# A graph convolution on one core: 528 instead of 512 chunks of edges counted by source and type, one row buffer fewer, and the first ring additions and flush placed earlier

## The chip, the cores and the metric

The kernel runs on one core of a Trainium2 chip. A core has a matrix engine (TensorE, "PE" in the profile; its weight loads are listed apart as "PEld"), a vector engine (VectorE, "DVE"), a scalar engine (ScalarE, "ACT"), a general-purpose engine (GpSimd, "POOL") and a queue that does little else than issue transfers (SyncE, "SP"). They work at the same time and wait for each other through semaphores. Data lies in HBM, in the on-chip SBUF (128 partitions) and, for matmul results, in PSUM. The metric is the device time of one execution in microseconds (us); lower is better.

## The reference

A graph has 12,500 nodes with 128 float32 features each, and 200,000 directed edges with a type from 0 to 3. The node features are normalized and cut at zero. Every edge takes the row of its source, multiplies it by the 128 x 128 matrix of its type, adds that type's bias, and the results are summed per destination node and added to the input.

```python
xs = x[src]                                   # x here: relu(layernorm(x))
for i in range(4):
    mask = (edge_types == i)[:, None]
    msgs = msgs + jnp.where(mask, xs @ W[i] + b[i], 0.0)
out = jax.ops.segment_sum(msgs, dst, num_segments=N)
return x + out
```

Two facts of the inputs shape the kernel. The edges come sorted by destination, and the destination is drawn as 12,500 times a squared uniform number: low nodes have very many edges each, high nodes few.

## The kernel before, in words

The 200,000 edges are cut into 1563 chunks of 128. Because the multiplication is linear, the kernel first sums source rows per destination and type, and multiplies by the four matrices afterwards. It sums in two ways.

*The dense head.* The first `C0` = 512 chunks belong to the lowest 1392 nodes or so. For each such node the kernel counts how many edges come from which source and of which type. `count` (lines 938 to 992) does this with one-hot matrices. A "slot" is one chunk's share of one node. For every slot DVE makes two one-hots (lines 957 and 961 or 965) and PE multiplies them (line 983) into a 128 x 396 table of counts in PSUM; ACT copies it out (line 989). `multiply` (lines 1021 to 1072) then multiplies the counts with the whole table of normalized rows. The table has 98 blocks of 128 rows, each row as three bf16 parts (768 bytes), and streams from HBM through `STREAM` = 4 buffers of six blocks (576 KB each, line 1029, issued by SP). Nodes with few edges share a "unit" of up to three, told apart by powers of 256 in the counts. A batch has up to `UB` = 27 units, 12 columns each (324 columns), and every batch streams the whole table: 98 x 3 = 294 matmuls at line 1033. Four small matmuls per tail (line 1047) apply the type matrices, and DVE adds the result to `acc` (line 1066).

*The gathered rest.* The other 1051 chunks go in groups of `G` = 16. For each chunk POOL gathers 128 rows of the table by an indirect transfer (line 544) into a tile `hm` of the pool `rows` (12 buffers, two chunks each). DVE makes a one-hot of destination and type (line 561). PE adds the rows up in three matmuls per chunk (line 578, one for each bf16 part), ACT copies the sums (line 581), PE applies the four type matrices (lines 596, 603, 605), and DVE adds each chunk's piece into a ring of 2048 node columns (`ring_adds`, lines 651 to 668, one addition per chunk at line 666). The first `RAW` = 3 groups are gathered from x itself (line 528) while the table is still being made, and their sums wait in `raw_sums`.

*The order.* Until the table stands, a scheduler of the language orders the instructions. The loop at line 1304 fixes the order of PE, DVE and ACT by hand. For every group `gi` it issues the next group's gathers, and walks through the present group in parts of two chunks; before each part it puts in dense work until the share that `pace` (line 1079) asks for is reached. `pace` counts matmul columns and spreads the dense columns evenly, so that every group from the fourth to the one before the last full one has the same number of columns, own and dense together. DVE's small pieces (`side`: ring additions, one-hots, table preparation) are spread over the same parts. The additions of the raw groups join `side` at lines 1309 and 1310, one raw group in each of the groups 4, 5 and 6 (counted from zero).

*Flushes.* When all edges of a stretch of nodes have passed, `put_out` (line 704) moves that stretch from the ring to the output: PE transposes (line 691), DVE adds x, SP stores; the first flush adds the ring's first columns to `acc`. `goes` (lines 741 to 744) chooses the group after which each flush goes; the first can go no earlier than after group `RAW` + 2 = 5.

*The tables of slots.* `prep_dense` and `make_slots` (line 793) work out on the chip, while the row table is made, which rows of which chunk belong to which slot. They treat the dense chunks in blocks of 128 (`DENSE` = 4 blocks), and the slots in pieces of up to 512 columns; for each piece and block DVE makes a one-hot (line 816).

Of the kernel before, what the change touches and what calls it, by code (L numbers as in the profile page):

```python
# [35 lines left out]
F32 = mybir.dt.float32  # L36
# [12 lines left out]
P = 128  # L49
# [3 lines left out]
SG = 4  # L53
WIN = 32
ROOM = 6
C0 = 512
UB = 27
MANY = 16
HB = 6
# [7 lines left out]
RAW = 3  # L67
# [7 lines left out]
def kernel(  # L75
# [22 lines left out]
    assert NT * WIN == P  # L98
    DENSE = -(-C0 // P)
    E0 = C0 * P  # L100
    TM = T - C0
    BM = -(-TM // P)
    BR = 16
    BC = -(-TM // BR)
    assert C0 % 16 == 0 and C0 <= NFULL

# [13 lines left out]
    FULL = (TM - sum(ends_in)) // G  # L120

    def window_of(c):

        m = min((c - C0) // G, FULL)
        end = (C0 + (m + 1) * G if m < FULL else T) * P / E
        a_node = E * ((end**2 + 1 / N) ** 0.5 - end)
# [19 lines left out]
    for i, n in enumerate(sizes_of):  # L146
# [4 lines left out]
        of = alone[3 * many_at : 3 * (many_at + n1)]  # L151
# [79 lines left out]
    flag = const.tile([P, 1], I32, name="flag")  # L231

    mid = ExitStack()
    hpool = mid.enter_context(tc.tile_pool(name="rows", bufs=12))
    opool = mid.enter_context(tc.tile_pool(name="onehots", bufs=2))
    spool = mid.enter_context(tc.tile_pool(name="typed", bufs=2))
    x_ps = mid.enter_context(tc.tile_pool(name="x_ps", bufs=4, space=PSUM))
# [28 lines left out]
    QB = max(2, DENSE)  # L266

    def prep_edges(m0, m1, prep, QB):
        n = m1 - m0
        c0, c1 = C0 + m0 * P, min(C0 + m1 * P, T)  # L270
        si = prep.tile([P, QB, P], I32, name="si")
        edge_rows(si, src, c0, c1, 0)
        ty = prep.tile([P, QB, P], I32, name="ty")
        edge_rows(ty, etype, c0, c1, NT)
        di = prep.tile([P, QB, P], I32, name="di")
        edge_rows(di, dst, c0, c1, N - 1)
        if c1 > NFULL and REST:
            r = (NFULL - c0) % P
            nc.sync.dma_start(
                di[r : r + 1, n - 1, REST:], dst[E - (P - REST) :].rearrange("(p e) -> p e", p=1)  # L280
            )
        sf = prep.tile([P, QB, P], F32, name="sf")
        nc.vector.tensor_copy(sf[:, :n], si[:, :n])
        pg = x_ps.tile([P, QB, P], F32, name="pt")
        for q in range(n):
            nc.tensor.transpose(pg[:, q, :], sf[:, q, :], ident)
        nc.scalar.copy(srcT[:, m0 % TURN : m0 % TURN + n, :], pg[:, :n, :])
        nc.vector.tensor_copy(head[:, m0:m1], di[:, :n, 0])
        rel = prep.tile([P, QB, P], F32, name="si")
        for q in range(n):  # L290
            nc.vector.tensor_scalar(rel[:, q, :], di[:, q, :], head[:, m0 + q : m0 + q + 1], None, ALU.subtract)
        key = prep.tile([P, QB, P], F32, name="sf")
        for q in range(n):
            nc.vector.scalar_tensor_tensor(
                key[:, q, :], ty[:, q, :], span[:, m0 + q : m0 + q + 1], rel[:, q, :], op0=ALU.mult, op1=ALU.add
            )
        pk = x_ps.tile([P, QB, P], F32, name="pt")
        for q in range(n):
            nc.tensor.transpose(pk[:, q, :], key[:, q, :], ident)
        nc.scalar.copy(keyT[:, m0 % TURN : m0 % TURN + n, :], pk[:, :n, :])  # L300
        nc.vector.tensor_reduce(ends[:, m0:m1, 0], rel[:, :n], AX.X, ALU.max)
        nc.vector.tensor_sub(ends[:, m0:m1, 0], ends[:, m0:m1, 0], span[:, m0:m1])
        nc.vector.tensor_reduce(ends[:, m0:m1, 1], rel[:, :n], AX.X, ALU.min)
# [34 lines left out]
    nc.vector.memset(warm, 0.0)  # L338
    nc.scalar.activation(warm, warm, AF.Sqrt)
    prep_edges(0, 1, prep, QB)  # L340


# [386 lines left out]
    def due(jb):  # L729
# [7 lines left out]
    sizes = [G] * FULL + ([r] if r else []) + ends_in  # L737
    starts = [sum(sizes[:i]) for i in range(len(sizes))]

    final = len(sizes) - 1  # L740
    goes = [
        next((i for i in [*range(RAW + 2, FULL), final - 1] if starts[i] + sizes[i] >= c), final)
        for ja, _, c in flushes
    ]

# [520 lines left out]
    for g in groups:  # L1266
# [17 lines left out]
    raw_adds = [  # L1284
        ring_adds(m * G, G, lambda i, m=m: raw_sums[:, (m * G + i) * win_raw : (m * G + i + 1) * win_raw], win_raw)
        for m in range(RAW)
    ]
# [9 lines left out]
    rows = gather(RAW * G, G)  # L1297
# [6 lines left out]
    for gi, (t0, g) in list(enumerate(zip(starts, sizes)))[RAW:]:  # L1304
        q = (t0 + 8 * G) // P
        if (t0 + 8 * G) % P < G and 2 <= q < BM:
            steps = [prep_steps(q, later)]
        side = [lambda of=of: ending.append(put_out(*of)) for of in soon]
        if gi > RAW and raw_adds:
            side += raw_adds.pop(0)  # L1310
        soon = list(flushing)
        flushing.clear()
        now = rows, oh
        if steps:
            side.append(lambda of=steps[0]: next(of, None))
        if gi < final:
            rows = gather(starts[gi + 1], sizes[gi + 1])
        parts = -(-g // HG)
        when = min(2, parts - 1)
        todo = len(side) + G + 1 + (G if finish else 0)  # L1320
        for j, part in enumerate(sum_up(t0, g, *now, gi >= FULL)):
            late, tails[:] = list(tails), []
            while work and spent < pace(gi, part):
                spent = next(work, None)
                if spent is None:
                    work = None
            for f in late:
                f()
            if checks and next(checks[0], None) is None:
                checks.pop(0)  # L1330
            if j == 0:
                if finish:
                    next(finish[0])
                if gi < final:
                    oh, made = one_hots_of(starts[gi + 1], sizes[gi + 1])
                    side += made
            if j == when:
                if finish:
                    next(finish.pop(0))
                side.append(lambda: [ending.pop(0)() for _ in list(ending)])  # L1340
                side += adds
                adds.clear()
                todo = min(todo, len(side) * parts // max(1, parts - 1 - j))
            left = todo * (parts - 1 - j) // parts - (0 if j >= when else todo - len(side))
            while side and len(side) > left:
                side.pop(0)()
            for _ in range(2):
                if leaving:
                    leaving.pop(0)()
        assert not side  # L1350
        if work is None and not dense_out:
            while tails:
                tails.pop(0)()
            for check in checks:
                for _ in check:
                    pass
            dense_out = True
            assert goes[0] < gi

            counting.close()  # L1360
            leaves = [(ja, min(ja + OT, NDT)) for ja in range(0, NDT, OT)]
            late = [(ja, jb) for (ja, jb, _), i in zip(flushes, goes) if i >= gi]
            outp = mid.enter_context(tc.tile_pool(name="outs", bufs=len(leaves + late)))
            for ja, jb in leaves + late:
                seen_out[ja] = fetch(ja, jb)
            second = []
            for ja, jb in leaves:
                leaving.append(lambda ja=ja, jb=jb: second.append(leave(ja, jb, acc, ja * P)))
                if len(leaving) > 1:
                    leaving.append(lambda: second.pop(0)())  # L1370
            leaving.append(lambda: second.pop(0)())
        for (ja, jb, _), i in zip(flushes, goes):
            if i == gi < final - 1:
                flushing.append((ja, jb, True))
        if gi == final:
            for l in leaving:
                l()
            assert not ending and not flushing and not soon
            next(finish[0])
            next(finish.pop(0))  # L1380
            for ahead in (True, False):
                for (ja, jb, _), i in zip(flushes, goes):
                    if i >= final - 1 and (i < final) == ahead:
                        put_out(ja, jb, False)()
                for add in adds:
                    add()
                adds.clear()
        if gi == FULL - 3:
            assert q == BM - 1
            check_chunks()  # L1390
        if dense_out and not checked:
            checked = True
            check_all()
# [127 lines left out]
```

## Time and profile before

| | |
|---|---|
| median of three runs | 1667.36 us (1666.21 to 1667.64) |
| the profiled execution's own time | 1663.02 us |
| its span in the trace | 1661.2 us |
| granted TensorE clock, mean | 0.958 |
| PE busy | 1417.4 us, 85% |
| DVE busy | 1014.6 us, 61% |
| POOL busy | 1030.6 us, 62% |
| ACT busy | 446.9 us, 27% |
| moved by DMA | 308.90 MB, 186 GB/s |

The profile is one execution as the hardware recorded it. A row of the costliest groups names the line of the kernel, the engine, the operation, what it writes and reads, its shape and how often it ran; after the bar come the busy time in us, the mean length of one instruction in ns, and the idle time of the engine before such instructions with what ended it. Matmuls overlap, so the mean length of one is longer than the distance from one to the next. "issue" is time in which an engine waited for nothing that the profile shows. The chain of waits follows the execution back from its last instruction. In a timeline a row is one instruction or a run of equal ones: its start, its length, and in square brackets the idle time before it. In a table by windows each window has its length, then busy time and number of instructions of PE, PEld, DVE, ACT and POOL, then the granted clock, the DMA engines' busy share and the data rate.

The time falls into stages: until about 113 us the row table and the tables of slots are made; until about 180 us the raw groups are added up and the first batch is counted; from there to about 1606 us gathered groups and dense work run interleaved, one group in about 24 us; the rest is the closing groups, the last flushes and the store.

### The profile page before, as it was taken

To read this page: it belongs to the slowest core of one execution; us is meant where nothing else is said; L and a number is where in the kernel's file an instruction comes from. 1 tells how busy PE (TensorE), PEld (TensorE's weight loads), DVE (VectorE), ACT (ScalarE), POOL (GpSimd) and SP (SyncE) were. 2 spreads that over 40 slices of the span, in tenths; PEclk is the share of its full clock that TensorE was granted. 3 is DMA by queue.
4 is the path that set the end of the run, shared out by engine and by line. 5 is a ranking of instruction groups with operands and counts; after the bars stand their busy time and mean duration, and the time that the engine had idled before them with its cause. 6 is when DMAs were issued, how large, how long until landed. Compare 5 with 4: busy or idle time off the path is not lost.

```text
span 1661.2 us, 32454 instructions
## 1 busy us (share of the span) xinstructions
PE 1417.4 (85%) x10984; PEld 921.7 (55%) x10984; DVE 1014.6 (61%) x5305; ACT 446.9 (27%) x1095; POOL 1030.6 (62%) x1078
## 2 busy tenths in 40 slices
PE   3868798988888889898979899998898889898975
PEld 1336565655555556565555556565565555555644
DVE  6982877647474746574756565666466556563433
ACT  5694222221212122222222222222222222222111
POOL 6435666666666666666666666666666666666562
PEclk9986899999999999999999999999999999999997
DMA  6552476665665656656656565665565556556652
GB/s 204 168 197 75 153 229 194 205 212 185 196 205 182 200 176 211 204 184 199 202 168 199 185 194 187 198 194 188 190 205 185 193 185 193 185 181 192 206 165 63
DMA packets 136761, 308.90 MB, mean 186 GB/s; under 512 B 25899, under 2 KB 78813, under 8 KB 136590
## 3 DMA queue, kind: packets, MB, share of 16 engines
q1 hardware_dynamic: 86909, 204.98, 37.8%
q0 software_dynamic: 49680, 101.81, 20.4%
q8 instruction: 86, 1.41, 0.3%
q14 instruction: 86, 0.70, 0.1%
HBM read 290.65 MB, written 16.04 MB: 185 GB/s over the span
## 4 chain that ended last, share of the span: by engine, by line
PE 74%; DVE 11%; issue 9%; another core or an unknown queue 2%; ACT 1%; DMA 1%; POOL 0%; SPq 0%; DVEq 0%; ACTq 0%; POOLq 0%
PE pa L1033 43%; PE pt L983 11%; PE ps L578 6%; PE py L605 6%; DVE o L957 2%; DVE o L965 2%; PE pt L1047 1%; DVE ring L666 1%; DVE oh L561 1%; PE ps L635 1%; PE py L596 1%; PE pt L691 1%; DVE stt L440 1%; POOL hm L544 0%
## 5 line engine op out<-in xcount | busy, mean ns | idle before, releaser
L544 POOL DMA_INDIRECT hm<-htab,srcT x1003 | 975.0, 972 | 565.5 <-issue 230.9
L1033 PE MATMUL pa<-counts,hs 128*128 128x324 fp8e4 (+1 forms) x5292 | 963.3, 305 | 79.2 <-issue 69.7
L1033 PEld LDWEIGHTS <-hs 128*128 128x128 bf16 x5292 | 492.3, 97 | 353.9 <-issue 132.7
L957 DVE TENSOR_SCALAR o<-iota_n,hkT 128x392 bf16<-128x392 f16 x1167 | 385.0, 330 | 75.2 <-PE pt L983 30.2
L983 PE MATMUL pt<-o,o 128*128 128x396 bf16 x1167 | 369.5, 337 | 40.3 <-DVE o L965 21.4
L989 ACT CAST counts<-pt 128x396 int32<-128x396 f32 x476 | 228.5, 493 | 479.4 <-PE pt L983 149.0
L561 DVE TENSOR_SCALAR oh<-iota_b,keyT 128x56 bf16<-128x56 bf16 (+8 forms) x1003 | 172.8, 260 | 294.6 <-PE ps L578 101.3
L581 ACT COPY sb<-ps 128x224 f32<-128x224 f32 (+8 forms) x251 | 99.4, 397 | 544.5 <-PE pt L983 172.5
L578 PE MATMUL ps<-oh,hm 128*128 128x56 bf16 (+8 forms) x3009 | 192.1, 197 | 38.9 <-issue 32.7
L666 DVE TENSOR_TENSOR ring<-ring,py 128x14 f32 (+7 forms) x976 | 171.9, 176 | 84.4 <-remote 17.3
L578 PEld LDWEIGHTS <-hm 128*128 128x128 bf16 x3009 | 165.2, 99 | 100.4 <-issue 55.1
L965 DVE TENSOR_SCALAR o<-iota,loT 128x128 bf16<-128x128 bf16 x644 | 177.2, 275 | 0.0
L983 PEld LDWEIGHTS <-o 128*128 128x128 bf16 x1167 | 111.3, 98 | 98.9 <-issue 30.2
L965 DVE TENSOR_SCALAR o<-iota,loT,byT 128x128 bf16<-128x128 bf16 x417 | 142.0, 340 | 0.0
L605 PE MATMUL py<-sb,wsb 128*128 128x224 f32 (+7 forms) x488 | 128.3, 402 | 5.5 <-issue 5.3
L605 PEld LDWEIGHTS py<-sb,wsb 128*128 128x128 f32 x488 | 86.4, 190 | 32.9 <-issue 11.7
L528 POOL DMA_INDIRECT hx<-in_x_dram,srcT x48 | 50.1, 1044 | 36.8 <-DVE stt L440 13.1
L997 DVE COPY bi<-counts 128x27 int32<-128x27 int32 (+1 forms) x18 | 4.1, 225 | 107.2 <-ACT counts L989 60.5
L600 ACT CAST cnt<-py 128x224 bf16<-128x224 f32 (+7 forms) x61 | 24.1, 395 | 103.7 <-PE ps L578 35.6
L461 ACT ACTIVATE h<-hm,nmrt,rstdt 128x128 f32<-128x128 f32 x98 | 42.8, 492 | 0.9 <-issue 0.5
L490 PE MATMUL ps<-h,ident 128*128 128x384 f32 (+1 forms) x34 | 17.2, 591 | 15.7 <-issue 11.4
L596 PE MATMUL py<-oh,three 128*32 128x224 bf16 (+7 forms) x244 | 21.2, 311 | 7.6 <-issue 3.9
(234 smaller groups left out, 650.2 us busy)
## 6 DMA issues: line engine op xcount, KB each, us to landing
hs<-htab SPq DMA_DIRECT2D x288, 576.0 KB
hm<-htab,srcT POOLq DMA_INDIRECT x1003
htab<-h SPq DMA_DIRECT2D x32, 288.0 KB
xo<-in_x_dram SPq DMA_DIRECT2D x23, 256.0 KB
out_dram<-xo SPq DMA_DIRECT2D x23, 256.0 KB
hm<-in_x_dram SPq DMA_DIRECT2D x18, 192.0 KB
hs<-htab SPq DMA_DIRECT2D x18, 192.0 KB
hm<-in_x_dram SPq DMA_DIRECT2D x14, 168.0 KB
```

What stands on the lines that cost most here:

```text
L528: one = nc.gpsimd.indirect_dma_start(out=hm[:, i * D : (i + 1) * D], out_offset=None, in_=x, in_offset=bass.IndirectOffsetOnAxis(ap=srcf[: ...
L544: one = nc.gpsimd.indirect_dma_start(out=hm[:, (i - h0) * D3 : (i - h0 + 1) * D3], out_offset=None, in_=htab, in_offset=bass.IndirectOffse ...
L561: nc.vector.tensor_scalar(oh[:, i, :], iota_b[:, :K], keyf[:, at : at + 1], None, ALU.is_equal)
L578: nc.tensor.matmul(ps[:, i - i0, :], rows(i, c), oh[:, i, :], start=(c == 0), stop=(c == 2))
L581: nc.scalar.copy(sb[:, i0:i1].rearrange("p g t n -> p g (t n)"), ps[:, : i1 - i0, :])
L605: nc.tensor.matmul(py[:, :g, :], wsb[:, t, :], sb[:, :g, t, :], start=False, stop=(t == NT - 1))
L666: nc.vector.tensor_tensor(to, to, of(i), ALU.add)
L957: one = nc.vector.tensor_scalar(o2[:, k, :NB], iota_n, hkT[:, s : s + 1], None, ALU.is_equal)
L965: one = nc.vector.tensor_scalar(o1[:, k], iota_1, loT[:, s : s + 1], by, ALU.is_equal, ALU.mult)
L983: one = nc.tensor.matmul(pb, o1, o2, start=first, stop=last)
L989: nc.scalar.copy(counts[:, :, i * NT : (i + 1) * NT], pb.rearrange("p (b t) -> p b t", t=NT))
L1033: nc.tensor.matmul(pa[:, : 3 * nu * NT].rearrange("p (m v) -> p m v", m=3), hs[:, j - j0, c * D : (c + 1) * D], of, start=(j == 0 and c == 0),
```

## The change

`C0` goes from 512 to 528. All that follows from it is worked out by the kernel's planner:

| | before | after |
|---|---|---|
| gathered chunks (48 of them raw) | 1051 | 1035 |
| dense blocks of 128 chunks | 4 | 5, the last of 16 |
| dense nodes, slot columns | 1392, 1584 | 1480, 1672 |
| slots counted | 1167 | 1211 |
| units, and batches | 476 = 17 + 17 x 27 | 506 = 20 + 18 x 27 |
| matmuls at line 1033 | 5292 | 5586 |
| planner's columns, dense | 2,136,792 | 2,259,880 |
| planner's columns, gathered groups | 549,632 in 60 groups | 543,360 in 59 groups |
| columns per group | 44,774 | 47,513 |
| flushes, and the groups after which they go | 24: 5, 7, 8, 12 ... 66, 67 | 23: 3, 7, 11, 16 ... 65, 66 |

Beside it the pool `rows` has 11 buffers instead of 12. Two PSUM tiles of `prep_steps` get the size that is used (with five blocks the old size would be larger than a bank). `goes` may choose from group 3 on. And the additions of the raw groups join the side work one group earlier: those of two raw groups (32 additions) in group 3, those of the third in group 4.

```diff
-C0 = 512
+C0 = 528
...
-    hpool = mid.enter_context(tc.tile_pool(name="rows", bufs=12))
+    hpool = mid.enter_context(tc.tile_pool(name="rows", bufs=11))
...
-        pg = x_ps.tile([P, QB, P], F32, name="pt")
+        pg = x_ps.tile([P, n, P], F32, name="pt")
...
-        pk = x_ps.tile([P, QB, P], F32, name="pt")
+        pk = x_ps.tile([P, n, P], F32, name="pt")
...
-        next((i for i in [*range(RAW + 2, FULL), final - 1] if starts[i] + sizes[i] >= c), final)
+        next((i for i in [*range(RAW, FULL), final - 1] if starts[i] + sizes[i] >= c), final)
...
-        if gi > RAW and raw_adds:
-            side += raw_adds.pop(0)
+        for of in raw_adds[: RAW - 1 if gi == RAW else 1]:
+            side += of
+        del raw_adds[: RAW - 1 if gi == RAW else 1]
```

## The prediction

> **What bounds the kernel now.** I read the page first: engine shares, the chain of waits and the costliest groups.
>
> ```profile
> PE 1417.4 (85%) x10984; PEld 921.7 (55%) x10984; DVE 1014.6 (61%) x5305; ACT 446.9 (27%) x1095; POOL 1030.6 (62%) x1078
> ...
> PE 74%; DVE 11%; issue 9%; another core or an unknown queue 2%; ACT 1%; DMA 1%; POOL 0%; SPq 0%; DVEq 0%; ACTq 0%; POOLq 0%
> ...
> L544 POOL DMA_INDIRECT hm<-htab,srcT x1003 | 975.0, 972 | 565.5 <-issue 230.9
> L1033 PE MATMUL pa<-counts,hs 128*128 128x324 fp8e4 (+1 forms) x5292 | 963.3, 305 | 79.2 <-issue 69.7
> ...
> L957 DVE TENSOR_SCALAR o<-iota_n,hkT 128x392 bf16<-128x392 f16 x1167 | 385.0, 330 | 75.2 <-PE pt L983 30.2
> L983 PE MATMUL pt<-o,o 128*128 128x396 bf16 x1167 | 369.5, 337 | 40.3 <-DVE o L965 21.4
> ...
> L578 PE MATMUL ps<-oh,hm 128*128 128x56 bf16 (+8 forms) x3009 | 192.1, 197 | 38.9 <-issue 32.7
> L666 DVE TENSOR_TENSOR ring<-ring,py 128x14 f32 (+7 forms) x976 | 171.9, 176 | 84.4 <-remote 17.3
> ```
>
> TensorE carries the chain, but "issue" (nothing visible is waited for) has 9% of it. The next view is busy time by stretch; after each window: its length, then PE, weight loads, DVE, ACT, POOL, granted clock, DMA share and GB/s. The last two windows are one group (16 chunks) each.
>
> ```profile
> 60.00:105.00 45.00, 36.94 (x156) 15.23 (x154) 43.94 (x158) 35.61 (x90) 16.10 (x14) 1.00 0.51 168
> 152.00:180.00 28.00, 15.82 (x117) 8.76 (x117) 18.91 (x95) 9.49 (x24) 17.86 (x18) 0.80 0.31 85
> 280.00:560.00 280.00, 249.05 (x2040) 163.56 (x2039) 176.95 (x948) 63.48 (x160) 178.47 (x184) 0.98 0.61 196
> 1120.00:1400.00 280.00, 249.06 (x1949) 161.62 (x1948) 165.59 (x869) 69.73 (x159) 181.08 (x187) 0.99 0.60 190
> 551.40:572.10 20.70, 20.05 (x175) 13.33 (x174) 14.79 (x83) 3.88 (x11) 12.27 (x13) 1.00 0.64 198
> 572.10:596.10 24.00, 21.17 (x178) 13.54 (x177) 14.56 (x73) 6.51 (x16) 15.57 (x17) 1.00 0.60 190
> ```
>
> In the main stage PE is busy 249 of 280 us early and late, 89%. A group normally takes 24.0 us, but 20.7 us is possible: same work, PE 97% busy. So some 31 us per 280 are idle on PE. Where they lie is seen in the timelines of POOL (first) and PE (second).
>
> ```profile
> 583.58 1.02 POOL L544 DMA_INDIRECT hm<-htab,srcT  x1 [1.19 <-PE pt L983]
> 584.90 0.95 POOL L544 DMA_INDIRECT hm<-htab,srcT  x1 [0.31 <-issue]
> 586.15 0.94 POOL L544 DMA_INDIRECT hm<-htab,srcT  x1 [0.30 <-issue]
> 587.40 0.95 POOL L544 DMA_INDIRECT hm<-htab,srcT  x1 [0.30 <-issue]
> 589.57 0.94 POOL L544 DMA_INDIRECT hm<-htab,srcT  x1 [1.22 <-PE pt L983]
> ```
> ```profile
> 583.27 0.59 PE L1033 MATMUL pa<-counts,hs 128*128 128x324 fp8e4 x3 [0.90 <-issue]
> ...
> 585.48 0.33 PE L983 MATMUL pt<-o,o 128*128 128x396 bf16 x1
> 585.64 1.02 PE L1033 MATMUL pa<-counts,hs 128*128 128x324 fp8e4 x6
> 586.50 0.33 PE L983 MATMUL pt<-o,o 128*128 128x396 bf16 x1
> ...
> 589.31 0.45 PE L1033 MATMUL pa<-counts,hs 128*128 128x324 fp8e4 x2 [0.42 <-issue]
> ...
> 595.24 0.31 PE L1033 MATMUL pa<-counts,hs 128*128 128x324 fp8e4 x1 [0.41 <-issue]
> ```
>
> POOL makes four gathers 1.25 us apart, then waits 1.2 us: 589.57 - 583.58 = 5.99 us for four, 1.50 us each. PE's idle spells end at 583.27, 589.31 and 595.24, on the same beat of 6.0 us, just before POOL starts again. They stand before matmuls of L1033 that name no wait. PE and POOL share a beat; the question that decides the sign is whether extra PE work lengthens it or fills its idle part.
>
> ```profile
> POOL hm L544 <- issue: 230.9, 752, 0.6
> POOL hm L544 <- PE ps L578: 89.4, 66, 4.1
> ```
> ```profile
> 1613.32 0.95 POOL L544 DMA_INDIRECT hm<-htab,srcT  x1 [0.30 <-issue]
> ```
>
> 752 of the 1003 gathers wait only 0.31 us (230.9 / 752), a fixed step. After the table stream has ended a gather takes 0.95 + 0.30 = 1.25 us with no beat (last row). Formally POOL's longer waits end on PE, which frees a buffer.
>
> **The change, part by part.**
>
> *Gathers, 1003 to 987.* One group of 16 goes (60 become 59 between the raw ones and the closing ones). If the beat holds, 16 x 5.99/4 = **-24.0 us**. Had these gathers gone at 1.25 us, -20.0 us.
>
> *Dense work.* By the kernel's own list of units, 476 become 506 (batches 17 + 17 x 27 to 20 + 18 x 27), slots 1167 become 1211. `multiply` streams 98 x 3 = 294 matmuls per batch at 12 columns per unit: 30 x 12 x 294 = 105,840 columns more. From the rows above, six L1033 start within 586.50 - 585.64 = 0.86 us, 143 ns for 324 columns, so +46.8 us; 44 counts at 585.64 - 585.48 = 0.16 us give +7.0. The planner's columns per group rise from 44,774 to 47,513, 6.1%. Spread over 59 groups, 53.8 us is 0.91 us of PE work per group. The removed group's own 6,272 columns, at 143/324 ns each, take 2.8 us back: net +51.0 us of PE work. What is to hide it is the idle: 24.00 - 21.17 = 2.83 us per group in the last window. I take **0** for it, with ends 0 and +51.0 (at full cover and no cover). If the idle scales with the work, 51.0 / 0.89 = +57.3. I choose the near end because the beat is rigid while the matmul mix in it changes (2040 matmuls in one 280 us window, 1949 in another, busy 249.05 and 249.06) and because the 20.7 us group shows that PE alone can be faster. These rows do not exclude the far end.
>
> DVE makes two one-hots per slot; with the second put at the first's 330 ns, 44 x 0.66 = +29 us, less 16 ring additions x 0.176 = 2.8. It is busy 177 of 280 us, so 0 on the path; without that cover, +26. The nineteenth batch streams the whole table again, 98 blocks x 128 rows x 768 bytes = 9.6 MB, against 16 x 128 x 768 bytes = 1.6 MB of gathers fewer: +8.0 MB. At 0.190 MB per us that would be 42 us if the DMAs were the bound, but their busy share is 0.60: 0.
>
> *The fifth dense block in the prelude.* 528 chunks need five blocks of 128, so each piece of the slot tables takes five one-hots instead of four, 10 more in all, and the pieces grow by 88 columns each.
>
> ```profile
> L816 DVE TENSOR_SCALAR sel<-qa,cidx 128x512 f16<-128x512 f16 (+1 forms) x16 | 4.8, 335 | 0.1
> ```
>
> 10 x 0.335 = 3.4 us at most, plus wider pieces and preparation (640 columns for 512), about 2. DVE is busy 43.94 of 45 us at 60 to 105, so nothing hides them: **+5** (0 to 9). The extra small loads at the start and 24 matmuls on PE lie beside this and cost 0; without that cover, +4 by 24 x 0.16.
>
> *Raw additions.* 32 instead of 0 in group 3, 16 in group 4, none in groups 5 and 6. 32 x 0.176 = 5.6 us of DVE where it makes the first slots (18.91 of 28 us busy at 152 to 180) and PE (15.82) waits for those; the same 5.6 come off later, where DVE has room. **+2.5** (0 to 5.6). Queued behind these additions on DVE are the one-hots of group 4 and of the first counts; PE's counts and L578 wait for them.
>
> *First flush after group 3 instead of 5.* The same flush work, 0; it can collide with the above, within its range (up to +1, and -1 if it leaves the ring free sooner).
>
> *First batch, 20 units instead of 17.* Six slots more before any `multiply` can run, 6 x 0.66 = 4.0 us on DVE if nothing lies beside it; other counts and one-hots do, so I take **+1.5** (0 to 4).
>
> *`rows` 12 to 11 buffers.* In the main stage gathers run 24 chunks, 24 x 1.50 = 36 us, ahead of their matmuls, now 22: no gather data is waited for, 0. While the table is made the same pool holds x blocks, loads start one block later; at the end two gathers wait longer, 2 x 1.25: **+2.5** (0 to 5). A loop with a fixed delay of 36 us and 22 chunks instead of 24 would be slower (rival C).
>
> *Smaller PSUM tiles in `prep_steps`.* The same instructions: 0.
>
> Sum against the profiled execution (1663.0 us, of which the span is 1661.2): 1663.0 - 24.0 + 5 + 2.5 + 1.5 + 2.5 = 1650.5. It lies 4.3 us under the median of the three runs, 1667.36, so the forecast is **1655 us**, 0.7% faster. With the terms' own ends (all small ones at their lowest, or all at their highest and gathers at 1.25 us) it is 1642 to 1677.
>
> One rule of the Trainium skill speaks against it. "TensorE: Matmul & The Clock Gate", section on the array as 16 sub-arrays, gives TensorE an instruction queue of 64. A full queue would make the idle before a matmul without a wait the array's own backlog, and 1655 would become the time of rival A. The trace has PE's idle at such matmuls (0.90 us at 583.27) but cannot show the queue's depth.
>
> **The rivals.**
>
> A. *PE paces the beat* (slower). POOL's long waits end on PE, its buffers are full, and PE never waits for a gather: so PE's own work, with its 11%, sets the group. For it: the chain has 74% PE, and the work per group is planned equal, so a constant period is no proof of another pacemaker. Against it: the 20.7 us group, and idle that ends on one beat with POOL. Then +57.3 + 11.5 of the small terms on 1667.4: **1736 us**; at back-to-back rates, with 51.0, 1730. It decides once PE's work per beat exceeds what the idle can take: 0.91 us of 2.83 per group must fit.
>
> B. *The idle is half cover.* Half of the 51.0 is paid and the gathers save their 24.0: 1655 + 25 = **1680 us**, slower by 0.8%.
>
> C. *The shorter ring of buffers paces POOL* (slower). 24 chunks of 36 us become 22: a gather goes from 1.50 to 1.63 us, some 920 of them in the main stage cost +120 at the worst. For it: the waits end on freed buffers. Against it: the buffers are freed by PE's order, which also moves up. With a quarter of that, 1655 + 30 = **1685 us**.
>
> D. *Nothing measurable*: the 24.0 us saved and small terms at their upper ends, plus part of the dense work, cancel: **1667 us**.
>
> **How the numbers follow.** Forecast 0.47, A 0.30, B 0.10, C 0.07, D 0.06. Within 0.2% (3.3 us) is about what the runs cannot tell from no change. Faster is the forecast's share, 0.47; same 0.05; slower A, B, C and a little of D, 0.48. The range has to take in A, since more than 2 in 10 lies there: from 1642, the forecast's low end, to 1738, just past A. The forecast's own range is 1642 to 1677.
>
> **What would show it.** Right: L544 x987, L1033 x5586; POOL still four gathers in 6.0 us, a group still 24.0 to 24.2 us, PE busy 92% of a group (21.17 + 0.91 = 22.1 of 24.0 us); one beat group fewer; raw additions stretch the windows up to 180 us by under 6. Wrong by A: PE still 89% busy, and groups of about 25.5 us, with POOL waiting 1.6 instead of 1.2 us per four gathers. By C: gathers further apart with PE's share falling below 89%. What would make the prediction wrong above all is that the idle on the beat belongs to PE itself.

## The result and the profile after

The changed kernel takes 1650.7 us (median of four runs, 1648.91 to 1652.71) against 1667.5 us before (1666.21 to 1668.61): a ratio of 0.990, 95% interval 0.9885 to 0.9915. The forecast was 1655 us. The profiled execution took 1651.06 us, with a span of 1649.2 us.

From the page of the changed kernel: shares of the engines, the chain of waits, and the groups that answer to those shown of before.

```profile
PE 1457.4 (88%) x11293; PEld 958.5 (58%) x11293; DVE 1041.5 (63%) x5387; ACT 458.7 (28%) x1121; POOL 1011.6 (61%) x1062
...
PE 81%; issue 8%; DVE 8%; ACT 2%; DMA 1%; DVEq 0%; SPq 0%; POOL 0%; ACTq 0%
...
L544 POOL DMA_INDIRECT hm<-htab,srcT x987 | 954.7, 967 | 575.6 <-issue 226.0
L1033 PE MATMUL pa<-counts,hs 128*128 128x324 fp8e4 (+1 forms) x5586 | 1000.5, 304 | 50.2 <-issue 47.1
```

PE works 40 us more and the kernel is 12 us shorter: the "issue" idle ahead of L1033 fell from 69.7 to 47.1 us. The windows of the changed kernel (columns as before: PE, weight loads, DVE, ACT, POOL, granted clock, DMA share, GB/s):

```profile
152.00:180.00 28.00, 14.85 (x105) 6.86 (x103) 20.34 (x105) 9.06 (x23) 16.87 (x19) 0.68 0.31 83
280.00:560.00 280.00, 258.48 (x2167) 173.26 (x2167) 182.31 (x967) 67.75 (x172) 178.01 (x186) 1.00 0.68 209
1120.00:1400.00 280.00, 257.38 (x2025) 168.08 (x2024) 176.76 (x925) 69.41 (x160) 176.50 (x184) 0.99 0.65 197
```

PE is now busy 258.5 of 280 us, 92%, where it was 249.05. POOL's timeline has the same beat:

```profile
570.55 0.94 POOL L544 DMA_INDIRECT hm<-htab,srcT  x1 [1.35 <-PE ps L578]
571.80 0.95 POOL L544 DMA_INDIRECT hm<-htab,srcT  x1 [0.30 <-issue]
573.06 0.95 POOL L544 DMA_INDIRECT hm<-htab,srcT  x1 [0.30 <-issue]
574.31 0.95 POOL L544 DMA_INDIRECT hm<-htab,srcT  x1 [0.30 <-issue]
576.51 0.95 POOL L544 DMA_INDIRECT hm<-htab,srcT  x1 [1.26 <-PE pt L983]
```

576.51 - 570.55 = 5.96 us for four gathers, against 5.99 before. Line 603 runs once per gathered group, so its view by source line gives the groups' pace. The columns: count, shortest/median/longest in ns, first and last start in us. Before, then after:

```profile
L603 PE MATMUL py<-cnt,b x61: 230/283/338, 183.2 to 1627.6; 128*128 128x224 bf16 x9, 128*128 128x320 bf16 x9, 128*128 128x192 bf16 x8, 128*128 128x256 bf16 x8
```
```profile
L603 PE MATMUL py<-cnt,b x60: 243/283/522, 188.4 to 1613.8; 128*128 128x224 bf16 x9, 128*128 128x320 bf16 x9, 128*128 128x192 bf16 x8, 128*128 128x256 bf16 x8
```

The time splits at these two starts. Up to the first: 183.2 to 188.4, **+5.2**. Between: 1444.4 us in 60 steps (24.07 each) to 1425.4 in 59 (24.16 each), **-19.0**. After the last: 33.6 to 35.4, **+1.8**. Together -12.0 us, the difference of the spans.

### The profile page after: what moved, and what is told of

Read it like the earlier page. It is cut to its first block, busy times and chain, and to the rows that moved or that the text cites. A ratio compares the mean times of both kernels' runs of the same rounds, so it can differ in the third digit from the quotient of the medians.

```text
span 1649.2 us, 33169 instructions
## 1 busy us (share of the span) xinstructions
PE 1457.4 (88%) x11293; PEld 958.5 (58%) x11293; DVE 1041.5 (63%) x5387; ACT 458.7 (28%) x1121; POOL 1011.6 (61%) x1062
## 4 chain that ended last, share of the span: by engine, by line
PE 81%; issue 8%; DVE 8%; ACT 2%; DMA 1%; DVEq 0%; SPq 0%; POOL 0%; ACTq 0%
PE pa L1033 47%; PE pt L983 12%; PE py L605 7%; PE ps L578 7%; DVE o L957 1%; PE pt L1047 1%; PE ps L635 1%; PE py L596 1%; PE pt L691 1%; DVE oh L561 1%; DVE o L965 1%; DVE ring L666 1%; PE pt L857 1%; DVE stt L440 1%; PE pt L854 0%
## 5 line engine op out<-in xcount | busy, mean ns | idle before, releaser
L544 POOL DMA_INDIRECT hm<-htab,srcT x987 | 954.7, 967 | 575.6 <-issue 226.0
L1033 PE MATMUL pa<-counts,hs 128*128 128x324 fp8e4 (+1 forms) x5586 | 1000.5, 304 | 50.2 <-issue 47.1
L1033 PEld LDWEIGHTS <-hs 128*128 128x128 bf16 x5586 | 519.0, 96 | 325.1 <-issue 84.7
L957 DVE TENSOR_SCALAR o<-iota_n,hkT 128x392 bf16<-128x392 f16 x1211 | 401.2, 331 | 75.4 <-PE pt L983 30.6
L983 PE MATMUL pt<-o,o 128*128 128x396 bf16 x1211 | 378.4, 336 | 37.0 <-DVE o L965 20.0
L989 ACT CAST counts<-pt 128x396 int32<-128x396 f32 x506 | 242.1, 493 | 500.5 <-PE pt L983 172.1
L561 DVE TENSOR_SCALAR oh<-iota_b,keyT 128x56 bf16<-128x56 bf16 (+8 forms) x987 | 167.7, 261 | 265.6 <-PE ps L578 94.6
L666 DVE TENSOR_TENSOR ring<-ring,py 128x14 f32 (+7 forms) x960 | 167.7, 175 | 65.0 <-PE pa L1033 13.0
L983 PEld LDWEIGHTS <-o 128*128 128x128 bf16 x1211 | 114.8, 97 | 96.2 <-DVE o L965 27.4
L965 DVE TENSOR_SCALAR o<-iota,loT,byT 128x128 bf16<-128x128 bf16 x461 | 155.4, 337 | 0.0
L1047 PE MATMUL pt<-sd,wsb 128*128 128x81 f32 (+1 forms) x152 | 25.8, 325 | 4.6 <-issue 4.6
```

Of the source, the lines that this page charges most:

```text
L544: one = nc.gpsimd.indirect_dma_start(out=hm[:, (i - h0) * D3 : (i - h0 + 1) * D3], out_offset=None, in_=htab, in_offset=bass.IndirectOffse ...
L561: nc.vector.tensor_scalar(oh[:, i, :], iota_b[:, :K], keyf[:, at : at + 1], None, ALU.is_equal)
L666: nc.vector.tensor_tensor(to, to, of(i), ALU.add)
L957: one = nc.vector.tensor_scalar(o2[:, k, :NB], iota_n, hkT[:, s : s + 1], None, ALU.is_equal)
L965: one = nc.vector.tensor_scalar(o1[:, k], iota_1, loT[:, s : s + 1], by, ALU.is_equal, ALU.mult)
L983: one = nc.tensor.matmul(pb, o1, o2, start=first, stop=last)
```

## The experiments

Theory S (with G, its form in the first runs): the beat of the gathers sets the groups' pace, and PE's idle takes extra work up. Rival P is rival A of the prediction: PE's own work sets it. Rival M: the gain comes from the placement of the additions and the flush.

The runs stand in three sets, each beside runs of the kernel before, and that kernel did not take the same time in them: 1419.1 us in the first set, 1667.0 in the second, 1419.0 in the third. The records give the chip of the second and third set the same number, so this is no fixed property of that chip number; what differed is not known. I call the two the *24 us pace* and the *20 us pace*, by the length of a group. The prediction and the result above belong to the 24 us pace.

### First set (20 us pace)

`pe360`, the kernel before with

```diff
+                if j % 5 == 2 and j + 1 < NW:
+                    nc.tensor.matmul(pa[...], hs[:, j - j0, :D], of, start=False, stop=False)
```

> The kernel before, with one more L1033 matmul in 20 of the 97 blocks that may have one, in each of the 18 batches: 360 matmuls more, 18 x 20 x 143 ns = 51 us of TensorE work, as much as the change adds net; the sums then take those blocks' first part twice. Gathers, transfers and the vector engine's work are as before. Theory G (the beat of the gathers sets the main stage and TensorE's idle takes the work up): 1667 to 1675 us, groups still 24.0 to 24.3 us, PE busy 92% of them. Rival P (TensorE's own work sets it): 51 to 57 us more, 1718 to 1725 us, PE busy still 89%.

`g15`, the kernel before with

```diff
             for i in range(h0, min(h0 + HG, g)):
+                if i == G - 1:
+                    continue
```

> The kernel before with 15 instead of 16 gathers in each of the 61 full gathered groups: the sixteenth chunk's matmuls take the fifteenth's rows again, so its rows are left out of the sums. TensorE's work is unchanged. Theory G: 61 x 1.50 = 91 us less, 1570 to 1585 us, groups 22.5 us, PE busy 94%. Rival P: the same time as before, 1660 to 1668 us.

`bufs11`, the kernel before with

```diff
-name="rows", bufs=12
+name="rows", bufs=11
```

> The kernel before with 11 row buffers alone. My step: 0 in the main stage and up to 5 us in the table stage and the tail, 1667 to 1672 us. Rival C (22 chunks in flight instead of 24 slow the beat of the gathers): 30 us more or above, 1695 us and up to 1790, groups of 24.5 to 26 us.

`adds_back`, the changed kernel with

```diff
-    [*range(RAW, FULL), final - 1]
+    [*range(RAW + 2, FULL), final - 1]
...
-        for of in raw_adds[: RAW - 1 if gi == RAW else 1]:
-            side += of
-        del raw_adds[: RAW - 1 if gi == RAW else 1]
+        if gi > RAW and raw_adds:
+            side += raw_adds.pop(0)
```

> The changed kernel with the raw groups' ring additions and the first flush where they were (additions of one group in each of groups 4, 5 and 6, first flush after group 5). My step: this placement costs 2.5 us, so undoing it gives 1645 to 1651 us. Rival M (a good part of the gain is this placement and not the 16 gathers): 1656 to 1667 us.

Measured, each against 1419.14 us: `pe360` 1463.69 (ratio 1.0303, interval 1.0281 to 1.0324), `g15` 1417.78 (0.999, 0.998 to 1.0), `bufs11` 1421.14 (1.0015, 1.0001 to 1.003), `adds_back` 1461.45 (1.0302, 1.0288 to 1.0316). Theory G failed here in both of its tests, and the number expected of `adds_back` belonged to another pace. The timeline of POOL and a window of `bufs11`, which is the kernel before but for one buffer, show why:

```profile
560.21 0.94 POOL L544 DMA_INDIRECT hm<-htab,srcT  x1 [0.30 <-PE ps L578]
561.46 1.03 POOL L544 DMA_INDIRECT hm<-htab,srcT  x1 [0.30 <-issue]
562.80 0.95 POOL L544 DMA_INDIRECT hm<-htab,srcT  x1 [0.30 <-PE pt L983]
564.05 1.07 POOL L544 DMA_INDIRECT hm<-htab,srcT  x1 [0.30 <-issue]
565.42 0.95 POOL L544 DMA_INDIRECT hm<-htab,srcT  x1 [0.30 <-issue]
```
```profile
280.00:560.00 280.00, 275.20 (x2391) 189.69 (x2390) 205.30 (x1098) 77.27 (x187) 209.67 (x215) 0.99 0.75 228
```

There is no beat: gathers follow each other at 1.25 to 1.37 us without a long wait, and PE is busy 98%. The traces of `pe360` and `pe360b` hold 342 added matmuls, 19 in each of 18 batches, and not the 360 that were expected: the twentieth block would be the last one of the table, which the edit leaves out. That is 49 us of work at 143 ns each. Where PE has no idle time, these 342 cost 44.5 us, 130 ns each, and gathers left out save nothing. Here rival P holds. One buffer fewer costs 2.0 us, barely clear of noise, so rival C's loop is not there at this pace.

### Second set (24 us pace)

`pe360b` and `g15b` are `pe360` and `g15` again. `half` is the kernel before with

```diff
-            nc.sync.dma_start(hs[:, : j1 - j0, :], htab...[:, j0:j1, :])
+            jh = min(j0 + HB // 2, j1)
+            nc.sync.dma_start(hs[:, : jh - j0, :], htab...[:, j0:jh, :])
...
-                        hs[:, j - j0, c * D : (c + 1) * D],
+                        hs[:, (j - j0) % (HB // 2), c * D : (c + 1) * D],
```

and `c496` the kernel before with `C0 = 496`.

> The 360 extra matmuls again, to see whether the answer depends on the chip: the chip of the first four runs had no beat of 6 us (gathers 1.29 us apart, groups of 20.2 us, PE 97 to 100% busy) and paid 44.5 us. Theory S (where the beat is there, it paces the groups and PE's idle takes work up; where it is not, PE's work is paid in full): on a chip with groups of 24 us 0 to 8 us more, on one with groups of 20 us 44 us more. Rival P (TensorE's work is paid on either): 44 to 57 us more on both.

> One gather of 16 left out again (the sixteenth chunk takes the fifteenth's rows). Theory S: on a chip with the beat 61 x 1.50 = 91 us less, groups of 22.5 us; on one without it no change, as measured there (0.999). Rival P: no change on either.

> The kernel before with the stream of the table cut in half: each transfer brings three blocks of six, and the other three blocks' matmuls take the same rows again (half of the table is left out of the dense sums). TensorE's instructions are unchanged. If the stream makes the beat by sharing the DMA engines with the gathers: on a chip with groups of 24 us, gathers at 1.25 to 1.40 us and groups of 20.5 to 22 us, 120 to 200 us less. If the beat has another cause: within 10 us. On a chip without the beat: within 5 us either way.

> The kernel before with C0 = 496: 1019 gathers and 4998 instead of 5292 matmuls at L1033, one group more. Theory S: with the beat 20 to 26 us more (a group of 24.1), 1.2 to 1.6% slower; without it 294 x 124 ns = 36 us of matmuls and 44 counts x 0.16 = 7 us less, 2 to 3% faster, 1375 to 1390 us. Rival P: 42 to 60 us faster on both.

Measured, each against 1667.0 us: `pe360b` 1670.87 (1.0022, 1.0007 to 1.0036), `g15b` 1596.7 (0.9582, 0.9563 to 0.960), `half` 1669.8 (1.0016, 1.0002 to 1.003), `c496` 1692.85 (1.0153, 1.0135 to 1.0172). The same window of each, in this order:

```profile
280.00:560.00 280.00, 252.18 (x2084) 168.02 (x2083) 173.49 (x935) 62.88 (x161) 176.56 (x183) 0.99 0.64 195
```
```profile
280.00:560.00 280.00, 258.11 (x2166) 172.99 (x2167) 184.72 (x996) 66.93 (x170) 176.06 (x182) 0.99 0.67 203
```
```profile
280.00:560.00 280.00, 246.65 (x2027) 161.37 (x2026) 175.22 (x943) 62.32 (x160) 177.98 (x184) 0.99 0.48 135
```
```profile
280.00:560.00 280.00, 238.13 (x1934) 155.47 (x1934) 172.18 (x920) 62.69 (x158) 178.46 (x184) 0.96 0.62 185
```

POOL's column is the one that stays: 182 to 184 gathers in 280 us whether PE has more work (`pe360b`), a gather per group is left out (`g15b`), the stream brings half (135 GB/s instead of 196) or there is less dense work (`c496`). PE's column is what varies, from 238 to 258 us. The same 342 matmuls that cost 44.5 us at the other pace cost 3.9 here. Rival P is excluded at this pace. So are the bytes of the table stream as the cause of the beat: with half of them nothing got faster (the number of its transfers stayed the same). `c496` is the change's opposite and loses 25.9 us for 16 gathers more (its granted clock in the window is 0.96 instead of 0.98, but the gathers come as often). At this pace the sign of the change follows from the gathers; whether their number, their rows or their bytes count, these runs do not tell apart.

One size was off. `g15b` saved 70.3 us by 61 gathers, 1.15 us each instead of 1.50. The groups' view by line 603 (numbered 605 in that kernel) gives them 1377.1 / 60 = 22.95 us rather than 22.5:

```profile
L605 PE MATMUL py<-cnt,b x61: 230/283/521, 183.9 to 1561.0; 128*128 128x224 bf16 x9, 128*128 128x320 bf16 x9, 128*128 128x192 bf16 x8, 128*128 128x256 bf16 x8
```

What takes the missing 0.45 us per group was not tried.

### Third set (20 us pace)

`after2` is the changed kernel again, `adds_back2` is `adds_back` again. `short` is the kernel before with

```diff
-                    out=hm[:, (i - h0) * D3 : (i - h0 + 1) * D3],
-                    in_=htab,
+                    out=hm[:, (i - h0) * D3 : (i - h0) * D3 + D],
+                    in_=htab.rearrange("n (c d) -> (n c) d", c=3),
```

and `rows64` the kernel before with

```diff
-                    out=hm[:, (i - h0) * D3 : (i - h0 + 1) * D3],
+                    out=hm[:64, (i - h0) * D3 : (i - h0 + 1) * D3],
```

where the list of rows and both operands of the chunk's matmuls are cut to 64 partitions too.

> The changed kernel again, beside its variant without the earlier additions. Theory S: on a chip with groups of 24 us 0.988 to 0.992 of the kernel before; on one with groups of 20 us 1.025 to 1.035.

> The changed kernel with the raw groups' additions and the first flush where they were. My step: the earlier placement costs 2.5 us (0 to 5.6), so this is 0 to 5.6 us faster than the changed kernel on the same chip. Rival M: the placement brings part of the gain, and this is 4 us or more slower than the changed kernel.

> The kernel before with gathers of 256 bytes a row instead of 768 (the first third of the bytes, the same number of rows; the three matmuls of a chunk take the same part, so two parts of every row are left out). If the bytes of the gathers make the beat: with groups of 24 us before, gathers at 1.25 to 1.35 us and 100 to 200 us less. If the number of gathers or of rows makes it: within 10 us. On a chip without the beat: 0 to 10 us less.

> The kernel before with gathers of 64 rows instead of 128 (half of the edges of each gathered chunk are left out, and the chunk's three matmuls take 64 partitions; all instructions are as many as before). If the rows of a gather make the beat: with groups of 24 us before, 100 to 200 us less. If the number of gathers makes it: within 10 us, the four gathers in 6.0 us still there. If the beat is PE's own: within 10 us too. On a chip without the beat: 0 to 15 us less.

Measured, each against 1419.01 us: `after2` 1468.86 (1.0345, 1.0329 to 1.0362), `adds_back2` 1460.84 (1.0294, 1.028 to 1.0308), `short` 1417.74 (0.9989, 0.9977 to 1.0001), `rows64` 1502.96 (1.0596, 1.0578 to 1.0613).

At this pace the same change makes the kernel 3.5% slower. `short` and `rows64` were meant to tell what in a gather makes the beat; there was no beat to act on, so that stays open. `rows64` came out 84 us slower, on the other side of its expectation (see the end).

The placement of the additions costs 8.0 us here (1468.86 - 1460.84), and rival M is excluded at this pace. DVE's timeline shows the two orders: the instruction behind the longest wait of the early stage, and the first one-hot of the counts (line 957) behind that, first of `after2`, then of `adds_back2`:

```profile
140.99 1.40 DVE L666 TENSOR_TENSOR ring<-ring,xo 128x10 f32 x7 [20.55 <-ACT xo L1283]
...
142.30 0.36 DVE L957 TENSOR_SCALAR o<-iota_n,hkT 128x392 bf16<-128x392 f16 x1
```
```profile
137.37 0.28 DVE L319 CAST sf<-si 128x128 f32<-128x128 int32 x1 [18.19 <-DMA si<-in_src_dram]
...
139.99 0.32 DVE L957 TENSOR_SCALAR o<-iota_n,hkT 128x392 bf16<-128x392 f16 x1
```

In the changed order DVE's first instruction of group 3 is a ring addition, and it needs the raw sums that ACT copies at line 1283. In the old order the table preparation comes first and waits for its data until 137.37. So DVE stands idle in both orders, 20.55 and 18.19 us, and the wait itself is worth little: the counts' one-hots behind it start 2.3 us apart (142.30 and 139.99), and the instruction before the wait already ended 1.2 us later in `after2`. Most of the 8 us arises behind the wait. The first start at line 603 tells when the first gathered group is done:

```profile
L603 PE MATMUL py<-cnt,b x60: 231/283/483, 172.5 to 1441.1; 128*128 128x224 bf16 x9, 128*128 128x320 bf16 x9, 128*128 128x192 bf16 x8, 128*128 128x256 bf16 x8
```
```profile
L603 PE MATMUL py<-cnt,b x60: 231/283/482, 161.7 to 1430.9; 128*128 128x224 bf16 x9, 128*128 128x320 bf16 x9, 128*128 128x192 bf16 x8, 128*128 128x256 bf16 x8
```

From that one-hot to the first group's line 603 it takes 30.2 us in `after2` and 21.7 in `adds_back2`. In this time DVE makes 48 raw additions (8.65 us, with 1.8 us of idle among them) instead of 16 (2.96 us), and PE waits meanwhile for the one-hots that stand between and behind them. From the first group on both kernels take the same 1268.6 and 1269.2 us, so the placement acts at the start alone, 10.8 us in these traces.

The traces at the 24 us pace have the same two orders. The kernel before, then the changed kernel:

```profile
154.16 0.23 DVE L319 CAST sf<-si 128x128 f32<-128x128 int32 x1 [25.74 <-DMA si<-in_src_dram]
...
158.14 0.32 DVE L957 TENSOR_SCALAR o<-iota_n,hkT 128x392 bf16<-128x392 f16 x1
```
```profile
157.20 1.40 DVE L666 TENSOR_TENSOR ring<-ring,xo 128x10 f32 x7 [19.41 <-issue]
158.51 0.35 DVE L957 TENSOR_SCALAR o<-iota_n,hkT 128x392 bf16<-128x392 f16 x1
```

Here the counts' first one-hot comes only 0.4 us later than before; the other 4.8 of the early stage's +5.2 us lie behind it, up to line 603. Rival M's own run at this pace is missing, but the stage in which the placement acts got longer, not shorter. What undoing the placement would bring there was not measured. The changed kernel with the old placement is the candidate that could beat both kernels at the 24 us pace; at the 20 us pace the kernel before beats it by 2.9%.

## Why the prediction was right

The sum said -12.5 us against the profiled execution, and it was -12.0; the median moved by -16.8 where -12.4 was forecast. That the sum came out so near is in part luck: against the stages, the three early terms were 3.8 us too high, the buffers' 0.7 too high, and gathers and dense work 5.0 too favourable. The profiled execution of the kernel before ran 4.5 us under its median and that of the changed kernel 0.4 above its own, so 4.8 us of the medians' move stand in no trace. The upper end of 1677 does not follow from the ends that I listed: they give 1672, and 1676 with the 4 us of the small loads.

*Gathers, -24.0.* Right in kind: four gathers still take 6.0 us, a group 24.1 us, and one group is gone. The main stage gave -19.0: one group of 24.1 less, and 59 groups longer by 0.09 us each, +5.1. The counter-test `c496` gave +25.9 us for one group more.

*Dense work, 0.* Right at this pace. PE's busy share rose to 92%, as said, and `pe360b` measured the cover by itself: 49 us of added PE work cost 3.9 us. The 20.7 us group that I leaned on came after one of 30 us (line 603 starts at 521.50, 551.25 and 572.01 us), so it made up for lost time; `pe360b` carries the argument, not that group. At the other pace there is no cover and rival A's event happens: `after2` is 49.9 us slower, where its price was 51.0 of PE work and 11.5 of small terms on a base of 1667. In the rule of the Trainium skill that I named ("TensorE: Matmul & The Clock Gate", the array as 16 sub-arrays, with a queue of 64) the idle ahead of matmuls without a wait could have been the array's backlog. `pe360b` shows that it was not: a backlog would not take up 49 us. The queue's depth itself no run here shows.

*Prelude +5, raw additions +2.5, first batch +1.5.* Together 9.0; the stage up to the first group's line 603 measured +5.2, and the split was wrong. I said that nothing hides the fifth block, because DVE is busy from 60 to 105 us. But DVE waits 25.74 us after that, and the counts' first one-hot behind the wait comes 0.4 us later, not 5. The other 4.8 us fall where the raw additions and the first batch lie, priced at 4.0; the traces do not part these two. The raw additions were right in kind, DVE time for which PE waits, and too cheap: I took 2.5 of their 5.6 us. `adds_back2` against `after2` makes the placement 8.0 us at the 20 us pace, above even the 5.6; 1.8 us of idle among the additions come on top of their length.

*`rows` with 11 buffers, +2.5.* The end of the kernel measured +1.8, the last flushes included; `bufs11` alone cost 2.0 us at the other pace. The beat with 11 buffers (5.96 us) is that with 12 (5.99), so rival C is not there at either pace.

Rival B is excluded by `pe360b` at this pace. Rival A was right about another pace: the chance of 0.30 that I gave it was not about the mechanism of this trace but, as it turned out, about when the kernel is run.

## What to carry to other kernels

When two engines idle on one beat, add work to one and take it from the other, alone, before changing the balance: 342 spare matmuls and one gather less per group told in two runs what the waits in the trace could not, since those waits ended on PE and PE still did not set the pace. Measure such a balance more than once: this change is worth -1.0% at one pace and +3.5% at another, by the same program. An instruction that is moved ahead of work for which another engine waits can cost its full length there, and the idle around it.

## What was not expected of the hardware

*Two paces of one program.* The kernel before took 1667 us in one set of runs and 1419 in others. What is equal in the two traces are the parts: a gather 0.95 us with 0.30 between two, and six L1033 in 0.86 us. What differs is the long wait after four gathers. The granted clock does not tell the paces apart: it is 0.98 between 280 and 560 us in the kernel before, and 0.99 in `bufs11`. Nor is the wait POOL's alone. In the kernel before, PE resumed at 583.27 and POOL at 583.58, and between them ACT and DVE:

```profile
583.34 0.34 ACT L581 COPY sb<-ps 128x224 f32<-128x224 f32 x1 [1.68 <-PE pt L983]
```
```profile
583.46 0.32 DVE L957 TENSOR_SCALAR o<-iota_n,hkT 128x392 bf16<-128x392 f16 x1 [1.05 <-PE pt L983]
```

From 300 to 1300 us POOL has 158 waits of over 0.6 us there, and 84 of them end within 0.5 us after PE has resumed from 0.3 us or more of idle. In the traces at the 20 us pace none does. So "the beat of the gathers" says what the time goes by, not what makes the beat.

The updates of the semaphore that PE raises come bunched at the 24 us pace and not at the other. Distances between successive updates, and the share of them under 0.1 us (300 to 1300 us in each trace):

```
kernel      25%       median    75%       under 0.1 us
before      0.076 us  0.726 us  1.49 us   34%
after       0.076 us  0.728 us  1.48 us   35%
pe360b      0.076 us  0.732 us  1.49 us   34%
bufs11      0.427 us  0.699 us  1.20 us    0%
after2      0.427 us  0.764 us  1.20 us    0%
```

The traces at the 24 us pace also hold far fewer updates of all semaphores together: 10,013 in the kernel before, 29,015 in `bufs11` (of PE's own 1583 and 1655). So what a wait there is said to end on is less sure, and whether the recording has a part in the pauses is not shown. Whether the bunching makes the beat or has a common cause with it is open too. Excluded at the 24 us pace are PE's amount of work, the bytes of the stream, and one row buffer fewer.

*Matmuls of 64 rows among those of 128.* In `rows64` a chunk pair's six short matmuls cost more than with 128 rows. Its PE timeline, and that of `bufs11`:

```profile
570.58 0.33 PE L983 MATMUL pt<-o,o 128*128 128x396 bf16 x1
570.75 0.59 PE L1033 MATMUL pa<-counts,hs 128*128 128x324 fp8e4 x3
571.18 0.33 PE L983 MATMUL pt<-o,o 128*128 128x396 bf16 x1
571.44 0.33 PE L578 MATMUL ps<-oh,hm 64*128 64x56 bf16 x6
571.70 1.03 PE L1033 MATMUL pa<-counts,hs 128*128 128x324 fp8e4 x6
```
```profile
569.79 0.59 PE L1033 MATMUL pa<-counts,hs 128*128 128x324 fp8e4 x3
570.22 0.34 PE L578 MATMUL ps<-oh,hm 128*128 128x64 bf16 x6
570.39 0.60 PE L1033 MATMUL pa<-counts,hs 128*128 128x324 fp8e4 x3
```

The six take 0.26 us to the next matmul instead of 0.17, and the matmul before them 0.26 (571.18 to 571.44) instead of 0.17 (L983 at 570.58, before an L1033). The trace has 492 such runs of short matmuls; two times 0.09 us for each are 89 us, and 84 were measured. The Trainium skill says that changing the tiling mode drains TensorE ("TensorEngine Tiling (Array Packing)", key properties); the trace agrees, with 0.09 us for each change.
